# A selective scan with its states taken two at a time: product, C load, accumulating transfer and sum

## Chip, cores and metric

The kernel runs on one core of one Trainium2 chip. The metric is device time in microseconds of one execution. The engines are TensorE (PE, with its weight loads PEld), VectorE (DVE), ScalarE (ACT), GpSimd (POOL) and SyncE (SP); 16 DMA engines serve the core.

## What is computed

The reference takes x of shape (16, 192, 64, 64) through four layers, each behind a normalisation: a small per-channel network that gives a likelihood, a shifted 1x1 convolution (five shifts), a two-dimensional selective scan, and a depthwise convolution with a 1x1 convolution and a batch norm. The change is in the scan:

```
dts, Bs, Cs = split(einsum('bkdl,kcd->bkcl', xs, x_proj_weight))     # 4 directions k, 16 states n
delta = softplus(einsum('bkrl,kdr->bkdl', dts, dt_projs_weight) + bias)
def step(h, inp):                      # over l = 0 .. 4095
    dA = exp(d[..., None] * A)
    h = dA * h + (d * u)[..., None] * Bt[:, :, None, :]
    y = einsum('bkdn,bkn->bkd', h, Ct)
ys = ys + xs * Ds                      # skip
y = sum of the four directions, each brought back to image order
```

The scan's input xn is x2 normalised, (x2 - gm) * rstd, and the kernel adds x2 itself to the scan's result.

## The kernel before, in words

The 16 images go through in eight pairs: 2 x 192 channels are 384 rows, three tiles (j) of 128 partitions. The first tile holds the first image, the third the second, and the middle one 64 rows of each.

A pair's scan (`scans`) runs over 48 steps t: tile j, direction k in the order 1, 3, 0, 2, and a quarter of the 4096 places (LC = 1024). Each step has 16 states n. One state of one step is a slot s, 768 a pair, 6144 in all. In a slot:

- ScalarE makes dA = exp(delta * A) (`decay`, three slots ahead; three buffers).
- TensorE spreads B's row over the partitions into PSUM (`spread`, two slots ahead; two buffers), two bf16 matmuls of 512 columns.
- VectorE multiplies it with du in place (`product`) and scans (`scan`, line 1020): h = dA * h + that.
- ScalarE copies the scan's last column to `state`.
- GpSimd multiplies h with C's row (line 1024). That row has been broadcast over the partitions by a DMA from SyncE's queue (`load_c`, two slots ahead, four buffers `cb`): 512 KB with runs of 4 KB. In the middle tile there are two transfers, one for each 64 partitions.
- Of every four states the first is added to the second by an accumulating DMA from GpSimd's queue (line 1026, 512 KB). The other three are added on TensorE by an identity matmul into PSUM (`add_up`, LATE = 4 slots after the scan), two fp32 matmuls of 512 columns each; the profile shows each fp32 matmul as two records. There are eight buffers of h.
- In the slot of each group's first state `add_up` adds images instead (`images`): for k = 0 the image of x2 (`xc`, a load of its own), the skip term (a diagonal matrix `skip` times xn) and the transposed directions `Xt`; for k = 2 and 3 what the directions before left in X or Xt.
- After the last state ScalarE copies the sum to X or Xt. This PSUM tile has one buffer, which the next step's delta (`step_rest`, at n = 4 and 10) uses too.

The instructions stand in an order written out by hand: each recorded call keeps its place in the program (line 66 in the profile is that recorder). Between these calls run pieces of the next image pair's first layers (`front`: statistics, `layer0`, `layer1`, `project`, `split`), about one piece a slot, paid by a credit; one slot of each step pays none. The eighth pair has no such work. `layer0` copies rows by SyncE to m0, takes tanh on ScalarE and matmuls on TensorE, through t1 and t2; its last matmul on t2 is issued a unit later.

After the scans, `layer3` normalises, convolves (taps on TensorE, GpSimd with ScalarE, and VectorE) and prepares the first step of the next pair (`begin`). Its tiles lie where the scans' buffers were; a tile `gap` of 25 KB keeps the images xp0 and xp1 beyond the scans' own buffers, so that both can be loaded before the scans end.

Pools that share a place in SBUF make the later writer wait for the earlier reader.

Of the kernel before, what the change touches and what calls it, by code (L numbers as in the profile page):

```python
# [11 lines left out]
F32 = mybir.dt.float32  # L12
# [31 lines left out]
LATE = 4  # L44
# [8 lines left out]
GAP = 25  # L53
# [53 lines left out]
def conv_preact_kernel(ctx: ExitStack, tc: tile.TileContext, a: dict):  # L107
# [43 lines left out]
    dtw = const.tile([32 + RD, K, NT, P], F32, name="t_dtw")  # L151
    for r in (0, 32):
        nc.sync.dma_start(out=dtw[r : r + RD], in_=a["dtw"])
# [11 lines left out]
    skip = const.tile([P, NT, P], F32, name="skip")  # L165
# [11 lines left out]
    for j in range(NT):  # L177
        nc.vector.tensor_scalar(skip[:, j, :], ident, dsk[:, 0, j : j + 1], None, ALU.mult)
# [126 lines left out]
    class Made:  # L305
        def __init__(self, n):
            def d(name, shape, dtype=F32):
                return dram.tile(shape, dtype, name=f"{name}{n}")

            self.x2 = d("x2_d", [NT * P, L])  # L310
            self.b = d("b_d", [P, L])
            self.c = d("c_d", [P, L])
            self.dt = d("dt_d", [K * RD, L])

            self.bp = d("bp_d", [K, BP, L], BF16)
            self.cp = d("cp_d", [2 * 2 * N, L])
            self.dtp = d("dtp_d", [2 * RD, L])
            self.gm = const.tile([P, NT], F32, name=f"gm{n}")
            self.rstd = const.tile([P, NT], F32, name=f"rstd{n}")

# [38 lines left out]
    def group_norm(E, st, stat, ps, gm, rstd, tiles=range(NT)):  # L359
# [50 lines left out]
        E.gps.tensor_tensor(rstd, d2, half, ALU.pow)  # L410


    def front(i, o, E, ps, deep):

        with tc.tile_pool(name="f_st", bufs=1) as stat:
            sts = [stat.tile([P, NT, 8, 6], F32, name=f"fst{n}") for n in range(3)]
# [35 lines left out]
            yield from layer1(o, E, ps, deep, sts[2], gms[1], rstds[1])  # L452
            yield from group_norm(E, sts[2], stat, ps, o.gm, o.rstd)
# [4 lines left out]
    def layer0(i, E, ps, deep, st, gm, rstd):  # L458
        with tc.tile_pool(name="l0w", bufs=1) as w_, tc.tile_pool(name="l0x", bufs=3) as xk, tc.tile_pool(
# [11 lines left out]
            def stream(chunks, no):  # L471
# [116 lines left out]
                for u, (ci, q) in enumerate(units):  # L588
# [13 lines left out]
                    t2 = tk.tile([GR, 2, 512], F32, name="t2", tag=f"t2{no}")  # L602
# [37 lines left out]
    def layer1(o, E, ps, deep, st, gm, rstd):  # L640
        with tc.tile_pool(name="l1w", bufs=1) as w_, tc.tile_pool(name="l1x", bufs=2) as xk, tc.tile_pool(
            name="l1r", bufs=6
# [24 lines left out]
            def load_r(c):  # L667
                if c < 8:
                    for j in range(NT):
                        xrs[c, j] = rk.tile([P, 512], F32, name="l1_xr")  # L670
                        E.sp.dma_start(
                            out=xrs[c, j], in_=row_tiles(x1_d)[:, j, 512 * c : 512 * c + 512]
                        )
# [23 lines left out]
            load_r(0)  # L697
# [4 lines left out]
            for c in range(8):  # L702
                at = 0
                for jo in range(NT):
                    p = ps("l1_p")
                    n, last = 0, 5 * len(INTO[jo]) - 1
                    for b, ji in INTO[jo]:
                        for s, (dy, dx) in enumerate(((0, 0), (0, 1), (0, -1), (1, 0), (-1, 0))):
# [11 lines left out]
                            if at == 8:  # L720
                                load_r(c + 1)
# [10 lines left out]
    def project(o, E, ps):  # L732

        with tc.tile_pool(name="pjw", bufs=1) as w_, tc.tile_pool(name="pjx", bufs=3) as xk:
# [21 lines left out]
            def done(to, c, m, p):  # L756
# [4 lines left out]
                E.sp.dma_start(out=to[:, 512 * c : 512 * c + 512], in_=r)  # L761
# [34 lines left out]
    def split(o, E):  # L796

        with tc.tile_pool(name="sp1", bufs=1) as one, tc.tile_pool(name="sp2", bufs=2) as two:
            nat = one.tile([P, L], F32, name="nat")
            E.sp.dma_start(out=nat[0:64, :], in_=o.b[0:64, :])  # L800
            E.sp.dma_start(out=nat[64:128, :], in_=o.c[0:64, :])
# [19 lines left out]
            for m in range(NC_):  # L821
# [3 lines left out]
                ct = two.tile([P, LC], F32, name="ct")  # L825
# [3 lines left out]
                E.sp.dma_start(out=o.cp[:, cs], in_=ct[64:128, :])  # L829
# [23 lines left out]

    def load_dt(sp, o, k, at):
# [9 lines left out]
    def make_delta(E, v, delta, dt, k, j):  # L864

        for h in range(2):
            rows = slice(32 * h, 32 * h + RD)
            E.pe.matmul(
                v[:, 512 * h : 512 * h + 512], dtw[rows, k, j, :], dt[rows, :], start=True, stop=True
# [4 lines left out]
    def load_first(o):  # L874
# [6 lines left out]
        return xn, load_bp(nc.sync, o, k, 0), dt  # L881

    def begin(o, loaded, psum):
# [3 lines left out]
        xn, bp, dt = loaded  # L887
        normalise(nc.vector, xn, xn, o.gm, o.rstd, 0)
        delta = over.tile([P, LC], F32, name="delta", tag="delta", bufs=2)
        make_delta(E, psum(), delta, dt, k, 0)  # L890
        du = over.tile([P, LC], F32, name="du", tag="du", bufs=2)
        nc.gpsimd.tensor_tensor(image(du), image(delta), columns(xn)[:, : LC // HW, :], ALU.mult)
        return xn, bp, delta, du

    def scans(i, o, p3, st3, begun, nxt):

        E = _Engines(tc, True)
        with ExitStack() as es:
# [5 lines left out]
            hp = pool("l2h", 8)  # L904
            da = pool("l2a", 3)
            cp = pool("l2c", 4)
# [5 lines left out]
            Xt = one.tile([P, L], F32, name="Xt")  # L912

# [7 lines left out]
            xns, xcs, state, bps, dts, made, ysum = {}, {}, {}, {}, {}, {}, {}  # L921
# [13 lines left out]
            def next_dt(t):  # L935
                if t < T:
                    j, k, at, first = todo[t]
                    dts[t] = load_dt(E.sp, o, k, at)

# [13 lines left out]
            def load_xc(t):  # L953
                if t < T and todo[t][1] == 0:
                    j, k, at, first = todo[t]
                    xcs[t] = one.tile([P, LC], F32, name="xc")
                    E.sp.dma_start(out=xcs[t], in_=row_tiles(o.x2)[:, j, at : at + LC])

            def load_c(s):
                t, n = divmod(s, N)  # L960
                j, k, at, first = todo[t]
                cb = cbs[s] = cp.tile([P, LC], F32, name="cb")
                src, row = (o.c, 64 + 16 * k) if k % 2 == 0 else (o.cp, 16 * (k - 1))
                for b, rows in {
# [4 lines left out]
                    r = row + N * b + n  # L969
                    E.sp.dma_start(  # L970
                        out=cb[rows, :],
                        in_=src[r : r + 1, at : at + LC].to_broadcast([rows.stop - rows.start, LC]),
                    )

            def step_rest(t):
# [5 lines left out]
                make_delta(E, v, delta, dts.pop(t), k, j)  # L981
# [28 lines left out]
            def scan(s):  # L1010
# [4 lines left out]
                dA, pbt, cb = dAs.pop(s), pbs.pop(s), cbs.pop(s)  # L1015
                back = k >= 2
                flip = slice(None, None, -1) if back else slice(None)
                h = hs[s] = hp.tile([P, LC], F32, name="h")
# [5 lines left out]
                E.gps.tensor_tensor(h, h, cb, ALU.mult)  # L1024
                if n % 4 == 1:
                    E.gps.dma_start(out=h, in_=hs[s - 1], accum_op=ALU.add)

            def add_up(s):

                t, n = divmod(s, N)  # L1030
                if s < 0:
                    return
                j, k, at, first = todo[t]
                if n % 4 == 0:
                    for c in range(LC // 512):
                        for w, v in images(t, n // 4 - 1, 512 * c):
                            E.pe.matmul(
                                ysum[t][:, 512 * c : 512 * c + 512], w, v, start=False, stop=False
                            )
                    return  # L1040
                h = hs.pop(s)
                if n % 4 == 1:
                    hs.pop(s - 1)
                if n == 1:
                    ysum[t] = py.tile([P, LC], F32, name="ysum", tag="ysum")
                for c in range(LC // 512):
                    cs = slice(512 * c, 512 * c + 512)
                    E.pe.matmul(
                        ysum[t][:, cs], ident, h[:, cs], start=(n == 1), stop=(n == N - 1)
                    )  # L1050
                if n == N - 1:
                    if k % 2:
                        E.act.copy(Xt[:, at : at + LC], ysum.pop(t))
                    else:
                        E.act.copy(rows_of(at, LC), image(ysum.pop(t)))

            def images(t, which, c):
# [3 lines left out]
                if k == 0:  # L1061
                    of = [
                        (ident, lambda: xcs[t][:, c : c + 512]),
# [9 lines left out]
                return [(w, v()) for w, v in of[which : which + 1]] if which >= 0 else []  # L1073
# [10 lines left out]
            xns[0], bps[0], *made[0] = begun  # L1084
            next_dt(1)
            for s in range(3):
                decay(s)
            for s in range(2):
                load_c(s)
                spread(s)  # L1090
            fr = front(*nxt, E, ps, False) if nxt is not None else iter(())
# [11 lines left out]
            for s in range(total):  # L1103
                t, n = divmod(s, N)
                j, k, at, first = todo[t]
                if s + 2 < total:
                    load_c(s + 2)
                if n == 2:
                    next_bp(t + 1)
                if n == 4:  # L1110
                    next_dt(t + 2)
                if n == 11:
                    load_xc(t + 1)
# [5 lines left out]
                if n == 4:  # L1119
# [8 lines left out]
                if (t + 1) % (K * NC_) == 0 and 5 <= n < 5 + NC_:  # L1128
                    norm_xn(j + 1, n - 5)
                if n > 4:  # L1130
# [317 lines left out]
```

## Time and profile before

| what | us |
|---|---|
| median of 3 runs | 27460.9 (27457.2 to 27462.78) |
| the profiled execution | 27459.08 |
| its span, first to last instruction | 27457.3 |
| busy: PE / DVE / ACT / POOL | 23391.4 / 23876.2 / 16298.7 / 20528.5 |
| first scan to last scan, pairs 1 to 7, mean | 2911.8 |
| the same, pair 8 | 2765.6 |
| last scan of a pair to first of the next | 342 |

A group's line gives the source line, engine, operation, what is written and read, shapes and count; then busy time, the mean of one in ns, and the engine's idle time just before such instructions with what ended it. A queue's line gives packets, MB, and the time its packets took as a share of 16 engines' span; q0 is GpSimd's queue, q1 SyncE's. A stretch's line gives start and end, length, busy time of each engine with its count, the granted TensorE clock, the share of the DMA engines and GB/s. The trace also records every DMA packet with its queue, size and time; where "packet records" are named, those are meant.

### The profile page before, as it was taken

The numbers are of one execution on the slowest core, as the hardware profiler recorded it, in microseconds if no ns is written. First come the engines' busy times: TensorE is split into PE (matmuls) and PEld (weight loads), VectorE is DVE, ScalarE is ACT, GpSimd is POOL, SyncE is SP. The second block draws the span as 40 slices with busy tenths as digits, with TensorE's granted clock in tenths as the row PEclk, the third lists the DMA queues.
The fourth block names the chain that finished last, engine by engine and source line by source line (L and its number), as shares of the span: only waits on it lengthen the run. The fifth ranks groups of instructions, "written<-read, shape, count | busy, mean of one in ns | idle before, by whom it ended". The sixth has DMA issues, their size and how long they took to land. (4 is left out here: it accounts for less than half of the span.)

```text
span 27457.3 us, 209986 instructions
## 1 busy us (share of the span) xinstructions
PE 23391.4 (85%) x58036; PEld 9490.8 (35%) x58036; DVE 23876.2 (87%) x15098; ACT 16298.7 (59%) x23334; POOL 20528.5 (75%) x10322
## 2 busy tenths in 40 slices
PE   8799888998789987999879988899878998766663
PEld 4343333333333332333334333333333333222221
DVE  0399998999889998999989999899989999899994
ACT  7388555874568644785447845587456864444443
POOL 2388876888778876888768887788877887677772
PEclk9899998999899998999989999999989999888886
DMA  4489874898668974898748987489856897467765
GB/s 102 132 221 226 220 226 131 224 219 218 181 182 225 222 213 142 221 224 224 218 138 220 227 219 220 138 222 218 219 173 188 225 222 215 137 190 194 202 186 245
DMA packets 2009593, 5471.86 MB, mean 199 GB/s; under 512 B 551592, under 2 KB 551816, under 8 KB 1991008
## 3 DMA queue, kind: packets, MB, share of 16 engines
q1 hardware_dynamic: 1783776, 4592.80, 57.7%
q0 software_dynamic: 221184, 805.40, 15.4%
q10 hardware_dynamic: 3456, 60.21, 0.5%
q8 instruction: 463, 7.59, 0.1%
q14 instruction: 714, 5.85, 0.1%
HBM read 3908.47 MB, written 340.96 MB: 155 GB/s over the span
## 5 line engine op out<-in xcount | busy, mean ns | idle before, releaser
L66 POOL TENSOR_TENSOR h<-h,cb 128x1024 f32<-128x1024 f32 x6144 | 14812.9, 2465 | 4331.0 <-ACT state L66 3637.1
L66 DVE TENSOR_TENSOR_SCAN h<-dA,state,pbt 128x1024 f32<-128x1024 f32 x4608 | 10807.6, 2345 | 727.0 <-ACT dA L66 119.9
L66 PE MATMUL ysum<-h,ident 128*128 128x512 f32 x18432 | 9280.1, 628 | 171.6 <-DMA h<-h 119.1
L66 DVE TENSOR_TENSOR pbt<-du,pbt 128x1024 f32<-128x1024 f32 x6144 | 7433.2, 1210 | 569.1 <-PE pbt L66 412.6
L66 ACT ACTIVATE dA<-delta,t_alog 128x1024 f32<-128x1024 f32 x6144 | 7034.6, 1146 | 6.5
L66 PEld LDWEIGHTS ysum<-h,ident 128*128 128x128 f32 x18432 | 3692.8, 202 | 4379.4 <-issue 3858.9
L66 ACT COPY state<-h 128x1 f32<-128x1 f32 x6144 | 1143.3, 186 | 6161.7 <-DVE h L66 6143.2
L66 PE MATMUL pbt<-bp,pick 96*128 96x512 bf16 x8192 | 2623.4, 404 | 1888.0 <-DVE h L66 1867.3
L66 DVE TENSOR_TENSOR_SCAN h<-dA,pbt 128x1024 f32<-128x1024 f32 x1536 | 3507.1, 2283 | 218.9 <-ACT dA L66 38.8
L66 PE MATMUL p<-t,wts 96*128 96x512 f32 x5376 | 2730.7, 605 | 162.8 <-ACT t L66 161.9
L66 PE MATMUL p<-m,wms 128*96 128x512 f32 (+1 forms) x5376 | 2662.4, 596 | 58.9 <-ACT t L66 44.7
L66 ACT ACTIVATE t<-p,bias 96x512 f32<-96x512 f32 x2688 | 1804.2, 678 | 1200.8 <-PE p L66 1187.6
L66 PEld LDWEIGHTS <-pick 96*128 96x128 bf16 x8192 | 673.7, 100 | 4795.4 <-DVE h L66 3281.0
L1209 POOL TENSOR_TENSOR l_g<-l_g,l_m 128x1024 f32<-128x1024 f32 x672 | 1627.5, 2423 | 620.9 <-ACT l_g L1205 474.7
L66 PE MATMUL l_p<-l_xp,w1s 128*128 128x512 f32 x3920 | 1883.3, 596 | 0.0
L66 PE MATMUL pbt<-bp,pick_mix 96*128 96x512 bf16 x4096 | 1270.1, 392 | 560.0 <-DVE h L66 555.5
L66 POOL DMA_DIRECT2D h<-h x1536 | 1356.3, 883 | 495.4 <-POOL h L66 419.3
L66 PEld LDWEIGHTS p<-t,wts 96*128 96x128 f32 x5376 | 1012.1, 191 | 1323.2 <-issue 883.4
L66 ACT ACT_TABLE_LOAD x1082 | 1388.2, 1283 | 19.0
L66 PEld LDWEIGHTS p<-m,wms 128*96 128x96 f32 (+1 forms) x5376 | 941.0, 177 | 811.8 <-issue 355.7
L1232 DVE SCALAR_TENSOR_TENSOR l_p<-xp,wc,l_p 128x1024 f32<-128x1024 f32 x768 | 990.4, 1290 | 223.8 <-PE l_p L1226 198.1
L66 ACT ACTIVATE m<-m,bias,sp 96x512 f32<-96x512 f32 x1344 | 1077.6, 802 | 87.0 <-DMA m<-l_xn 85.1
(241 smaller groups left out, 18647.7 us busy)
## 6 DMA issues: line engine op xcount, KB each, us to landing
cb<-cp_d SPq DMA_DIRECT2D x2048, 512.0 KB
cb<-c_d SPq DMA_DIRECT2D x2048, 512.0 KB
h<-h POOLq DMA_DIRECT2D x1536, 512.0 KB, 7.4
cb<-cp_d SPq DMA_DIRECT2D x2048, 256.0 KB
cb<-c_d SPq DMA_DIRECT2D x2048, 256.0 KB
m<-l_xn SPq DMA_DIRECT2D x3072, 128.0 KB
bp<-bp_d SPq DMA_DIRECT2D x384, 192.0 KB
rl<-x_d ACTq DMA_DIRECT2D x24, 2450.0 KB
```

The costliest lines, as they stand in the source:

```text
L66: return self._tc.keep_in_program_order(call(*args, **kw))
L1209: nc.gpsimd.tensor_tensor(g, g, m, ALU.add)
L1232: nc.vector.scalar_tensor_tensor(image(y if tap is TAPS[-1] else ps), window(j, 16 * c, 16, tap), factor(j, tap), image(ps), ALU.mult, ALU ...
```

## The change

States are taken in twos, u = s // 2:

- h and cb are tiles of 2 x 1024 columns (five of h, three of cb). Each scan writes its half. GpSimd multiplies both halves in one instruction after the second scan.
- C's rows are stored by quarters (`o.c`, `o.cp` get a leading axis of four), so that two states of a quarter lie together, and one load brings 8 KB runs for both. The middle tile still has two loads, of 64 partitions.
- Of every four states the first two are added to the last two by one accumulating transfer of 1 MB; TensorE adds two of four states. The sums come SUM = 6 slots after the scan, the second half one slot later, and images in the two slots between groups.
- For k = 0 the x2 image and the skip term become one image: since x2 = xn * std + gm, the diagonal is dsk + std (`gain`, made anew for each pair by one GpSimd and three ScalarE instructions), and gm is the bias of ScalarE's copy of the sum. `group_norm` makes std by one more GpSimd instruction. The loads `xc` are gone.
- Places in the slot order: dt loads at n = 8, delta at 7, du at 11, normalising the next xn at 4, 5, 8, 9, the slot without credit is 8.
- Room is made: dt's weights are loaded for each tile and direction (two loads of 12 rows), t2 takes the place of m0, `fst` has two tiles, `l1_xr` five with their loads spread out, `ct` one. xp1 lies ahead of a `gap` of 19 KB, over the place of the last h, of dA and of the first cb.

```diff
-LATE = 4
+SUM = 6
-GAP = 25
+GAP = 19
...
-                    t2 = tk.tile([GR, 2, 512], F32, name="t2", tag=f"t2{no}")
+                    t2 = m0[:GR]
...
+    def load_dtw(sp, k, j):
+        w = over.tile([32 + RD, P], F32, name="dtw", tag="dtw", bufs=2)
+        for r in (0, 32):
+            sp.dma_start(out=w[r : r + RD, :], in_=a["dtw"][:, k, j, :])
+        return w
...
-            hp = pool("l2h", 8)
+            hp = pool("l2h", 5)
             da = pool("l2a", 3)
-            cp = pool("l2c", 4)
+            cp = pool("l2c", 3)
...
-            def load_c(s):
-                t, n = divmod(s, N)
+            def load_c(u):
+                t, n = divmod(2 * u, N)
                 j, k, at, first = todo[t]
-                cb = cbs[s] = cp.tile([P, LC], F32, name="cb")
+                cb = cbs[u] = cp.tile([P, 2 * LC], F32, name="cb")
...
                     r = row + N * b + n
+                    two = src[at // LC, r : r + 2, :].rearrange("r l -> (r l)").unsqueeze(0)
                     E.sp.dma_start(
-                        out=cb[rows, :],
-                        in_=src[r : r + 1, at : at + LC].to_broadcast([rows.stop - rows.start, LC]),
+                        out=cb[rows, :], in_=two.to_broadcast([rows.stop - rows.start, 2 * LC])
                     )
...
-                h = hs[s] = hp.tile([P, LC], F32, name="h")
+                u, of = divmod(s, 2)
+                if of == 0:
+                    hs[u] = hp.tile([P, 2 * LC], F32, name="h")
+                h = hs[u][:, LC * of : LC * of + LC]
...
                 E.act.copy(v, h[:, 0:1] if back else h[:, LC - 1 : LC])
-                E.gps.tensor_tensor(h, h, cb, ALU.mult)
-                if n % 4 == 1:
-                    E.gps.dma_start(out=h, in_=hs[s - 1], accum_op=ALU.add)
+                if of:
+                    E.gps.tensor_tensor(hs[u], hs[u], cbs.pop(u), ALU.mult)
+                    if u % 2:
+                        E.gps.dma_start(out=hs[u], in_=hs[u - 1], accum_op=ALU.add)
...
+                turn = (s - SUM - 3) % 4
+                if turn < 2:
+                    t, n = divmod(s - SUM - turn, N)
+                    if t < 0:
+                        return
+                    u = (s - SUM - turn) // 2
+                    if n == 3 and turn == 0:
+                        ysum[t] = py.tile([P, LC], F32, name="ysum", tag="ysum")
                     for c in range(LC // 512):
+                        cs = slice(512 * c, 512 * c + 512)
+                        E.pe.matmul(
+                            ysum[t][:, cs],
+                            ident,
+                            hs[u][:, LC * turn + 512 * c : LC * turn + 512 * c + 512],
+                            start=(n == 3 and turn == 0),
+                            stop=(n == N - 1 and turn == 1),
+                        )
...
+                            elif k == 0:
+                                E.act.activation(
+                                    rows_of(at, LC),
+                                    image(ysum.pop(t)),
+                                    AF.Identity,
+                                    bias=o.gm[:, j : j + 1],
+                                )
...
-                        (ident, lambda: xcs[t][:, c : c + 512]),
                         (skip[:, j, :], lambda: xns[j][:, at : at + 512]),
...
+            E.gps.tensor_tensor(gain, dsk[:, 0, :], o.std, ALU.add)
+            for j in range(NT):
+                E.act.activation(skip[:, j, :], ident, AF.Copy, scale=gain[:, j : j + 1])
...
-                if s + 2 < total:
-                    load_c(s + 2)
+                if s % 2 == 0 and s + 2 < total:
+                    load_c(s // 2 + 1)
...
+            xp1 = gap.tile([P, S, S], F32, name="xp1")
             gap.tile([P, GAP * 256], F32, name="gap")
             diag = xk.tile([P, NT, PE_TAPS, P], F32, name="diag")
-            xps = [xk.tile([P, S, S], F32, name=f"xp{j}") for j in range(NT - 1)] + [X]
+            xps = [xk.tile([P, S, S], F32, name="xp0"), xp1, X]
```

## The prediction, made before the result was known

> **What bounds the kernel now.** I read first the page's queues and costliest groups, then busy time by stretch, then what VectorE (DVE) waited for, last the end of one pair. A "slot" is one state of one step: one product and one scan on VectorE. There are 768 in a pair and 6144 in all.
>
> ```profile
> q1 hardware_dynamic: 1783776, 4592.80, 57.7%
> q0 software_dynamic: 221184, 805.40, 15.4%
> ...
> L66 POOL TENSOR_TENSOR h<-h,cb 128x1024 f32<-128x1024 f32 x6144 | 14812.9, 2465 | 4331.0 <-ACT state L66 3637.1
> L66 DVE TENSOR_TENSOR_SCAN h<-dA,state,pbt 128x1024 f32<-128x1024 f32 x4608 | 10807.6, 2345 | 727.0 <-ACT dA L66 119.9
> L66 PE MATMUL ysum<-h,ident 128*128 128x512 f32 x18432 | 9280.1, 628 | 171.6 <-DMA h<-h 119.1
> L66 DVE TENSOR_TENSOR pbt<-du,pbt 128x1024 f32<-128x1024 f32 x6144 | 7433.2, 1210 | 569.1 <-PE pbt L66 412.6
> ...
> L66 POOL DMA_DIRECT2D h<-h x1536 | 1356.3, 883 | 495.4 <-POOL h L66 419.3
> ```
>
> A slot costs VectorE 1.21 + 2.33 = 3.55 us whatever else happens, and the change touches neither instruction. GpSimd (POOL) idled 4331 us before its h*C product, most of it waiting for the scan, so that product is not the bound.
>
> The next view is busy time by stretch: the three channel tiles (256 slots each) of the second pair, then of the eighth, which has no next image to prepare. After the stretch and its length come PE, PEld, DVE, ACT and POOL, the granted clock, the share of the DMA engines and GB/s.
>
> ```profile
> 4457.00:5436.00 979.00, 899.25 (x2285) 370.36 (x2286) 911.05 (x558) 745.64 (x1104) 788.50 (x403) 0.96 0.82 226
> 5436.00:6400.00 964.00, 894.50 (x2289) 369.76 (x2288) 906.80 (x547) 682.61 (x1007) 812.40 (x419) 0.98 0.95 224
> 6400.00:7363.00 963.00, 816.38 (x2021) 323.06 (x2019) 911.79 (x564) 470.82 (x681) 751.33 (x381) 0.95 0.77 223
> 23981.00:24902.00 921.00, 623.84 (x1410) 226.78 (x1411) 887.32 (x519) 402.25 (x585) 697.13 (x336) 0.87 0.67 195
> 24902.00:25825.00 923.00, 632.40 (x1426) 233.22 (x1425) 888.84 (x521) 401.37 (x584) 699.21 (x337) 0.87 0.79 194
> 25825.00:26746.00 921.00, 635.41 (x1432) 234.07 (x1431) 887.49 (x524) 394.63 (x581) 696.08 (x341) 0.86 0.67 196
> ```
>
> The reader sees that without a next image VectorE is 96% busy and a slot takes 921/256 = 3.60 us; with one, slots take 3.82, 3.77 and 3.76. From first scan to last, the first seven pairs take 2911.8 us on average and the eighth 2765.6. Of the 146 us between them, 66.5 are VectorE's own work for the next image (72 statistics at 0.68, 24 sums at 0.73). So 2911.8 - 2765.6 - 66.5 = 80 us a pair, 0.10 a slot, is waiting that a better order could remove: 560 us in seven pairs is the ceiling of any gain in the scans, and the floor of a slot is 3.60 + 0.09 = 3.69. The second tile already fills the DMA engines to 0.95.
>
> ```profile
> DVE pbt L66 <- PE pbt L66: 412.6, 553, 4.2
> ...
> DVE h L66 <- ACT dA L66: 158.7, 491, 2.7
> ...
> DVE h L66 <- DMA h<-h: 137.6, 90, 5.9
> ```
>
> VectorE's largest wait in the scans is for TensorE's spread of B. So TensorE, 92 to 93% busy in the first two tiles, is the second bound.
>
> **Part by part.** *Sums on TensorE.* Eight of 16 states (12 before) reach TensorE: 18432 records become 12288. Four that follow each other took 1.88 us in the timeline, 0.43 apart, so 6144 x 0.43 = 2640 us of TensorE go, 0.43 a slot of some 3.6; the dropped x image takes 384 records, 165 us. That empties the queue in front of the spread, and the 413 us of waits should go. What is late next is VectorE itself (floor 3.69) where nothing else binds.
>
> *Accumulating transfers.* They stay 1536 but carry 1 MB: 805 MB become 1611. A 4 KB packet of this queue took 341 ns on average in the packet records (a C-load packet 159 in the median). A slot has two on each DMA engine; doubled, +0.68 us of each engine's time per slot. No packet of 8 KB is accumulated in this trace: between 1.9 and 2.1 times 341; I take 2.0. GpSimd's issue (0.88 us) stays the same in number; if rows are cut into 4 KB pieces it may double, +0.22 us a slot of an engine that is 80 to 84% busy: 0 taken.
>
> *C loads in 8 KB runs.* Bytes are the same. The trace's nearest 8 KB packets (instruction fetch) took 309 ns at the tenth percentile against 2 x 159: -0.04 us a slot. The first packet of each transfer takes 300 to 450 ns instead of 159, and transfers halve: I take -0.16 us a slot where a tile has one load per state, -0.26 in the second, where it has two; bounds 0 and -0.35. The Trainium skill ("DMA: Bandwidth & Descriptors", section "Anatomy of one DMA") puts about 2 us of fixed cost on each transfer, measured on GpSimd's queue: 2 x 3.2 us become 4.4, an estimate, 2 us saved for two states, or 6 ms over the kernel were it on the path. The row says it isn't: GpSimd waited 605 us for C loads in all, 49 of it at the start of the second pair alone. I count only the engine time.
>
> *Where both meet.* The same page ("Issuing engines are not separate DMA queues") says that transfers issued by sync and by GpSimd run on the same 16 engines and interleave. This speaks against the change: work leaves TensorE for engines that the C loads need. Were the accumulating queue separate, I would take the floor everywhere (27020, below). The trace agrees with the page: in 20 us stretches of the second tile the shares never add up to much over 1.
>
> ```profile
> 2360.00:2380.00 20.00, 19.60 (x51) 8.08 (x49) 19.39 (x12) 18.15 (x27) 19.48 (x11) 1.00 1.06 238
> ```
>
> So I take 1.04 as full. Time of each engine per slot: first tile 0.82 x 3.82 = 3.13, + 0.68 - 0.04 - 0.16 = 3.61; over 1.04 that is 3.47, under the floor, but close. Third: 0.77 x 3.76 = 2.90, so 3.38; free. Second: 0.95 x 3.77 = 3.58, + 0.68 - 0.04 - 0.26 = 3.96, or 3.81 us a slot; without any saving 4.26, or 4.10. I take the middle, 3.95. The second tile is dear because each half of the partitions has its own load: its C packets took about 260 ns, against 205 in the other tiles. The eighth pair has 0.79 x 3.60 + 0.38 = 3.2 us and doesn't bind.
>
> *Sum of the scans.* First tile 3.82 to 3.73 (a little over the floor, since the engines are nearly full): -23 us. Second 3.77 to 3.95: +47. Third 3.76 to 3.70: -15. Together +9 a pair, x7 = +63 us.
>
> *End of a pair.*
>
> ```profile
> 4114.96 2.34 POOL L66 TENSOR_TENSOR h<-h,cb 128x1024 f32<-128x1024 f32 x1 [1.31 <-ACT state L66]
> ...
> 4127.25 1.03 ACT L66 COPY X<-ysum 128x1024 f32<-128x1024 f32 x1 [12.37 <-PE ysum L66]
> ```
>
> Before, the last sum was read 12.6 us after the last scan (which ended at 4114.66). Now the last two states come in one product (4.6 us: 2.36, and 2.14 per further 1024 columns, by the rows of 512 and 1024), then issue and landing (6.5 us in the eighth pair, + 8 x 0.33), then 8 records of 0.43 to 0.6: copy at about 4133. Nothing covers it, since statistics and group norm follow: +6 us x 8 = +48.
>
> *Waits that arise.* The sum now waits for a larger transfer, six slots after the scan instead of four. From scan to landing took 14 us (first tile) and 15 (second) in the median, against 15.1 allowed. Now: lag of GpSimd behind the scan 2.9 or 3.9 (medians of before), product 4.6, issue to landing 7.5 or 8.0 plus 2.7 for the bytes and up to 2.5 for interleaved C packets, in all 17.7 to 21.5, against 22.6. Behind a waiting sum on TensorE stands the next spread, but VectorE has two of those in hand, so under 4 us nothing is lost. Five h buffers let a scan start once the transfer of seven slots back has landed: 24 us. Only the second tile's tail reaches this; it is inside my 3.95.
>
> *At no cost:* t2 in m0's place makes SyncE's row copies wait for the closing matmul of the last unit; behind them stand C loads, which have some 18 us; TensorE passes that matmul in the same slot. dtw loads, gain and skip (one GpSimd and three ScalarE instructions a pair, under 2 us), std, and later delta and du (five slots of cover) go the same way. xp1 now lies over the last h, dA and C buffers, so its load starts with the last scan; it needs about 8 us and is first used 25 us later. If a cover failed, each would cost 2 to 8 us a pair, 16 to 64 us.
>
> Sum: 27459 (the profiled execution; span 27457.3; median of the runs 27460.9) + 63 + 48 = 27570.
>
> **Rivals.**
> A, likeliest (0.45): as summed; own range 27420 to 27800, the savings' bounds in the second tile. If rows are cut back into 4 KB (the change then doesn't do what it says), 4.10 there: 27459 + 7 x (84 - 38) + 48 = 27830.
> B, faster (0.33): the packet times are waiting rather than work, the engines overlap, and TensorE's relief counts everywhere. All slots at 3.70: 7 x 768 x (3.70 - 3.79) = -484, + 48: 27020; half of it 27265. For it: the second tile's first quarter (5436 to 5670) ran at 3.66 a slot with a DMA share of 0.97. Against it: the change asks for a tenth more than that.
> C, much slower (0.22): the engines bind in the first tile too and landings come after the 24 us of the h buffers, deciding once the landing is over 16 us from issue. Slots 3.95, 4.15, 3.76: 7 x (33 + 97) + 48: 28420; milder, 28000.
>
> **Numbers.** 27570; the range takes B to 27100 and C to 28150. Over or under 0.2% (55 us) is what a measurement can tell from no change. Faster: B and a little of A, 0.34; same: 0.13; slower: the rest of A, and C, 0.53.
>
> **What would show it.** ysum<-h x12288 and VectorE's waits for the spread below 100 us: the TensorE step. Queue 0 at about 30% of 16 engines: the transfer step; near 25%, B. DMA share of the second tile at 1.0 with slots over 3.85: the saturation; at 3.70, B. X copy 18 us after the last scan: the pair's end. Waits of scans for h<-h over 500 us: C. I am wrong if an 8 KB packet costs far from 2 x 341 ns, or if C packets shrink when their engines are full.

## The result and the profile after

The changed kernel takes 29257.2 us (median of 4 runs, 29233.0 to 29319.1) where the kernel before, in the same comparison, took 27459.1 (27452.0 to 27462.8). The ratio is 1.0659, with a 95% interval of 1.064 to 1.0677: 6.6% slower. The sign of the forecast held, its size (+111 us against +1798) did not; the time lies outside the range, past the price given to rival C.

First the page after: queues (packets, MB, share of 16 engines), then the groups that answer to those of before.

```profile
q1 hardware_dynamic: 1317296, 4543.25, 53.7%
q0 software_dynamic: 221184, 1610.71, 27.3%
...
L66 POOL TENSOR_TENSOR h<-h,cb 128x2048 f32<-128x2048 f32 x3072 | 14037.5, 4573 | 6252.2 <-ACT state L66 5242.4
L66 DVE TENSOR_TENSOR_SCAN h<-dA,state,pbt 128x1024 f32<-128x1024 f32 x4608 | 10808.8, 2346 | 2204.5 <-DMA h<-h 1644.9
L66 DVE TENSOR_TENSOR pbt<-du,pbt 128x1024 f32<-128x1024 f32 x6144 | 7425.6, 1209 | 455.5 <-PE pbt L66 280.6
...
L66 PE MATMUL ysum<-h,ident 128*128 128x512 f32 x12288 | 6717.0, 675 | 149.6 <-DMA h<-h 149.6
...
L66 POOL DMA_DIRECT2D h<-h x1536 | 1366.7, 890 | 495.4 <-POOL h L66 456.3
...
h<-h POOLq DMA_DIRECT2D x1536, 1024.0 KB, 11.6
```

Most instructions cost what they cost before or what the sum gave them: the scan 2346 ns (2345), the product of two states 4573 (forecast 4.6 us), the issue 890 (883), and 12288 records of sums, together 2563 us less (forecast 2640), though each takes longer (675 ns, 628 before; see the last section). What is new is what VectorE's scan waits for: 2204 us instead of 727, most of it the accumulating transfer. The waits name it in full (us in all, times, longest):

```profile
DVE h L66 <- DMA h<-h: 2065.4, 719, 11.9
...
DVE pbt L66 <- PE pbt L66: 280.6, 269, 4.9
...
ACT m L66 <- DMA m<-l_xn: 674.1, 196, 10.9
```

Before, the first was 137.6, the second 412.6, and the third stood at

```profile
ACT m L66 <- DMA m<-l_xn: 85.1, 70, 3.7
```

(ScalarE waiting for the rows of the next image that SyncE copies to m0). A scan waits for h<-h for one reason only: the h buffer that it writes is still being read or written by an accumulating transfer.

Busy time by stretch: the three tiles of the second pair, then of the eighth.

```profile
4714.00:5757.00 1043.00, 845.10 (x2011) 334.21 (x2012) 909.54 (x557) 747.50 (x1105) 767.20 (x275) 0.89 0.88 240
5757.00:6873.00 1116.00, 866.66 (x2016) 343.92 (x2015) 903.53 (x547) 688.58 (x1008) 790.31 (x289) 0.87 1.00 220
6873.00:7877.00 1004.00, 754.55 (x1748) 290.91 (x1746) 912.29 (x565) 471.33 (x683) 733.11 (x255) 0.86 0.88 247
25675.00:26643.00 968.00, 580.21 (x1136) 199.61 (x1136) 887.52 (x518) 402.17 (x588) 673.61 (x208) 0.72 0.80 217
26643.00:27567.00 924.00, 574.22 (x1152) 203.35 (x1153) 888.41 (x520) 400.38 (x584) 674.69 (x209) 0.74 1.02 227
27567.00:28544.00 977.00, 591.60 (x1163) 208.31 (x1163) 888.40 (x525) 393.98 (x583) 674.79 (x213) 0.72 0.80 215
```

VectorE's busy time (the third of the five) is unchanged to within 0.4%; its stretches are longer. Slots of pairs 1 to 7 take 4.08, 4.32 and 3.92 us by tile (3.84, 3.77, 3.76 before). All tiles but the second of the eighth pair lost, so saturation of the second tile can't be the whole. The last three lines hold the riddle: in the eighth pair the second tile has the fullest engines (1.02) and the fewest waits, slots of 3.61, while the first and third, at 0.80, take 3.78 and 3.82. VectorE's waits for h<-h in those three stretches:

```profile
DVE h L66 <- DMA h<-h: 53.6, 32, 4.0
...
DVE h L66 <- DMA h<-h: 4.2, 5, 1.3
...
DVE h L66 <- DMA h<-h: 60.1, 30, 4.1
```

The addresses of the h buffers in the built program explain it. A pool of five does not hand its buffers out in turn. In the eighth pair's first and third tiles, the source of an accumulating transfer (an even u) comes round four pairs of states later in 61 of 64 cases (counted by the scan that takes the buffer), its target six later; in the second tile both come round five later in 59 of 64. In pairs 1 to 7, the source has a round of four in 61, 44 and 53 of 64. With a round of four, the scan that takes the buffer starts five slots after the start of the scan that released the transfer: 5 x 3.6 - 2.35 = 15.6 us from that scan's end to the landing. With five it is seven slots: 22.8 us. Landings came 16.2, 19.8 and 16.4 us after the scan in the three tiles (medians). So the tile with the latest landings had room, and the others didn't.

One of these waits in the timeline (start, length, and in brackets the wait):

```profile
26109.17 2.35 DVE L66 TENSOR_TENSOR_SCAN h<-dA,state,pbt 128x1024 f32<-128x1024 f32 x1 [1.62 <-DMA h<-h]
```

By stretch, pairs 1 to 7 lost 7 x (3152.8 - 2911.8) = 1687 us between first and last scan, pair 8 103, what lies between and around them 17.

### The profile page after: what moved, and what is told of

The parts are those of the page before. It is cut to its first block, busy times and chain, and to the rows that moved or that the text cites. A ratio compares the mean times of both kernels' runs of the same rounds, so it can differ in the third digit from the quotient of the medians.

```text
span 29264.2 us, 182538 instructions
## 1 busy us (share of the span) xinstructions
PE 22247.3 (76%) x51508; PEld 8757.2 (30%) x51508; DVE 23846.3 (81%) x15095; ACT 16341.4 (56%) x23358; POOL 20043.6 (68%) x7266
## 3 DMA queue, kind: packets, MB, share of 16 engines
q0 software_dynamic: 221184, 1610.71, 27.3%
## 5 line engine op out<-in xcount | busy, mean ns | idle before, releaser
L66 POOL TENSOR_TENSOR h<-h,cb 128x2048 f32<-128x2048 f32 x3072 | 14037.5, 4573 | 6252.2 <-ACT state L66 5242.4
L66 DVE TENSOR_TENSOR_SCAN h<-dA,state,pbt 128x1024 f32<-128x1024 f32 x4608 | 10808.8, 2346 | 2204.5 <-DMA h<-h 1644.9
L66 DVE TENSOR_TENSOR pbt<-du,pbt 128x1024 f32<-128x1024 f32 x6144 | 7425.6, 1209 | 455.5 <-PE pbt L66 280.6
L66 PE MATMUL ysum<-h,ident 128*128 128x512 f32 x12288 | 6717.0, 675 | 149.6 <-DMA h<-h 149.6
L66 PE MATMUL pbt<-bp,pick 96*128 96x512 bf16 x8192 | 2878.2, 438 | 3561.5 <-DVE h L66 3502.8
L66 PEld LDWEIGHTS ysum<-h,ident 128*128 128x128 f32 x12288 | 2717.5, 222 | 3390.1 <-issue 3123.0
L66 PE MATMUL p<-m,wms 128*96 128x512 f32 (+1 forms) x5376 | 2980.5, 660 | 58.1 <-ACT lu L66 50.7
L66 PE MATMUL l_p<-l_xp,w1s 128*128 128x512 f32 x3920 | 2075.1, 649 | 11.8 <-POOL l_xp L66 11.8
L66 PE MATMUL p<-m,wts 96*128 96x512 f32 x2688 | 1492.7, 672 | 187.1 <-ACT m L66 185.8
L66 PE MATMUL p<-t,wts 96*128 96x512 f32 x2688 | 1477.4, 632 | 0.0
L66 ACT ACT_TABLE_LOAD x1082 | 1388.2, 1283 | 17.6
L66 PEld LDWEIGHTS <-pick_mix 96*128 96x128 bf16 x4096 | 360.2, 103 | 3295.3 <-DVE h L66 1832.5
L66 ACT ACTIVATE t<-p,bias 96x512 f32<-96x512 f32 x1344 | 900.4, 682 | 553.8 <-PE p L66 544.2
## 6 DMA issues: line engine op xcount, KB each, us to landing
h<-h POOLq DMA_DIRECT2D x1536, 1024.0 KB, 11.6
```

Source lines behind the costliest of these rows:

```text
L66: return self._tc.keep_in_program_order(call(*args, **kw))
```

## The experiments

Slots are us by tile, mean of pairs 1 to 7, then of pair 8.

| kernel | us | ratio to before, 95% | slots, pairs 1 to 7 | slots, pair 8 |
|---|---|---|---|---|
| before | 27459 | | 3.84 3.77 3.76 | 3.60 3.60 3.60 |
| after | 29257 | 1.064 to 1.0677 | 4.08 4.32 3.92 | 3.78 3.61 3.82 |
| e1, five in turn | 28449 | 1.0343 to 1.0374 | 3.91 4.20 3.79 | 3.59 3.62 3.60 |
| e9, rounds of 4 and 6 | 29570 | 1.0753 to 1.0782 | 4.08 4.38 3.97 | 3.82 4.00 3.81 |
| e5, e1 with C in 4 KB runs | 28560 | 1.0387 to 1.0415 | 3.96 4.23 3.82 | 3.59 3.60 3.60 |
| e6, e1 without half loads | 27789 | 1.0098 to 1.0129 | 3.93 3.83 3.79 | 3.59 3.60 3.60 |
| e8, e1 without the transfers | 27266 | 0.9914 to 0.9941 | 3.78 3.76 3.76 | 3.59 3.59 3.58 |
| e10, e1 with bytes of before | 27674 | 1.0066 to 1.0093 | 3.87 3.84 3.80 | 3.61 3.61 3.62 |
| e2, half transfer, two h read | 33485 | 1.2174 to 1.2211 | 4.73 4.73 4.81 | 4.66 to 4.70 |
| e3, before with t2 in m0 | 27534 | 1.0018 to 1.0037 | 3.84 3.81 3.77 | |
| e4, before with every second state transferred | 27978 | 1.0168 to 1.0202 | 3.84 4.00 3.79 | 3.63 3.64 3.62 |
| e7, before with eight in turn | 27386 | 0.9959 to 0.9982 | 3.81 3.77 3.76 | 3.60 3.60 3.60 |

**e1: the changed kernel, h buffers in turn**

```diff
-                    hs[u] = hp.tile([P, 2 * LC], F32, name="h")
+                    hs[u] = hp.tile([P, 2 * LC], F32, name="h", tag=f"h{u % 5}", bufs=1)
```

> The changed kernel, with one edit: its five h buffers are handed out strictly in turn. In the program of the changed kernel the source of an accumulating transfer is handed out again four pairs of states later (61 of 64 times in tiles 1 and 3 of pair 8), so its next scan may start only when a transfer of five slots back has landed; strictly in turn it is seven slots. Theory H (this hand-out is what costs): pair 8 returns to 3.60 us a slot in every tile (now 3.78, 3.61, 3.82), the scans' 2065 us of waits for h<-h fall below 300, tiles 1 and 3 with a next image go to 3.70 to 3.78 (now 4.08 and 3.92), in all 27400 to 27900. Theory D (the DMA engines are full): pair 8 changes, but with a next image tile 2 stays above 4.1 a slot (now 4.32) and tile 1 above 3.9, waits go over to the C loads and row copies; 28300 to 29000.

Measured: 28449.1, so 808 us of the 1798 come back with one argument. The wait for the transfer falls to an eighth; what grows in its place is the scans' wait for TensorE's read of the buffer (11.0 in the changed kernel) and ScalarE's for the row copies:

```profile
DVE h L66 <- PE ysum L66: 686.1, 430, 16.1
...
DVE h L66 <- DMA h<-h: 243.1, 74, 8.5
...
ACT m L66 <- DMA m<-l_xn: 1145.2, 295, 17.2
```

Pair 8 returns to 3.59 to 3.62 in all tiles, as theory H had it; the other pairs and the whole stay where theory D had them. The second tile of those pairs stays dear at 4.20. Its stretches in the second pair, by tile:

```profile
4595.00:5591.00 996.00, 825.79 (x2018) 328.63 (x2019) 909.25 (x558) 751.61 (x1110) 767.95 (x276) 0.92 0.92 252
5591.00:6663.00 1072.00, 858.86 (x2010) 337.78 (x2009) 904.39 (x546) 682.44 (x1004) 787.94 (x288) 0.89 1.02 230
6663.00:7631.00 968.00, 741.58 (x1743) 287.14 (x1742) 908.41 (x563) 471.01 (x681) 732.16 (x254) 0.88 0.90 254
```

The engines are full in the second tile, as forecast, and move fewer bytes a second there (230 against 252) than in the first. In the eighth pair, which has no row copies and no other loads for a next image, the same tile shows a share of 1.03 at slots of 3.62:

```profile
25858.00:26784.00 926.00, 575.46 (x1152) 204.26 (x1152) 888.62 (x521) 400.31 (x585) 675.80 (x209) 0.74 1.03 226
```

There the full engines just meet what is asked, 1.03 x 3.62 = 3.73 us a slot; with a next image it is 1.02 x 4.20 = 4.28, which fits in no slot of 3.7.

**e9: rounds of four and six in every tile**

```diff
-            hp = pool("l2h", 5)
+            he, ho = pool("l2he", 2), pool("l2ho", 3)
...
-                    hs[u] = hp.tile([P, 2 * LC], F32, name="h")
+                    hs[u] = (ho if u % 2 else he).tile([P, 2 * LC], F32, name="h")
```

> The changed kernel with its h buffers split: two for even u, three for odd u, so that in all tiles a source tile of an accumulating transfer comes round four pairs later and a target six. Theory (the round of the buffers is what the second 808 us are): tile 2 of the eighth pair, which had rounds of five and slots of 3.61, now gets rounds of four and slots of 3.80 or more (50 us or more); in pairs 1 to 7 the 20 of 64 groups of tile 2 and 11 of 64 of tile 3 that had five follow (4.37 and 3.95 a slot, 100 and 50 us). In all 29460 us. Rival (turns of five helped for another reason, such as which places in memory are written together): 29257 as the changed kernel, tile 2 of pair 8 at 3.61.

Measured: 29570.3, dearer than the change itself. The eighth pair, its second tile in the middle:

```profile
25860.00:26837.00 977.00, 580.99 (x1136) 199.55 (x1136) 887.44 (x519) 401.18 (x588) 672.51 (x208) 0.72 0.81 215
26837.00:27859.00 1022.00, 591.11 (x1152) 204.48 (x1152) 887.76 (x520) 400.26 (x584) 675.60 (x209) 0.71 0.95 206
27859.00:28832.00 973.00, 584.06 (x1158) 203.95 (x1159) 886.57 (x525) 393.61 (x582) 674.77 (x213) 0.72 0.80 215
```

The second tile went from 924 to 1022 us (slots 3.61 to 4.00) when only the round of its buffers changed; the first and third, which had rounds of four already, stayed. Second and third tile of the other pairs came to 4.38 and 3.97, as expected; that the whole is 110 us over the expected 29460 lies half in the eighth pair's second tile, which lost 98 us instead of 50. So the round causes the waits; that its price follows the landing is seen too: 5 x 4.00 - 2.35 = 17.6 us, near the 18.4 us at which landings came there.

**e5: C loads cut back to 4 KB runs, and e6: no loads of 64 partitions.** Both start from e1.

```diff
-                    two = src[at // LC, r : r + 2, :].rearrange("r l -> (r l)").unsqueeze(0)
-                    E.sp.dma_start(
-                        out=cb[rows, :], in_=two.to_broadcast([rows.stop - rows.start, 2 * LC])
-                    )
+                    for of in range(2):
+                        E.sp.dma_start(
+                            out=cb[rows, LC * of : LC * of + LC],
+                            in_=src[at // LC, r + of : r + of + 1, :].to_broadcast(
+                                [rows.stop - rows.start, LC]
+                            ),
+                        )
```

> The kernel with five buffers strictly in turn (28449 us; tile 2 at 4.20 us a slot with a next image), and its C loads again in runs of 4 KB: two transfers into the halves of the same buffer. Theory R: in tile 2, where each half of the partitions has its own load[...] (a C packet of 8 KB took 565 to 575 ns there, two of 4 KB 500 in the kernel before with doubled accumulation); tile 2 returns to 4.0 and the whole to 28000 to 28200. Rival: half as many transfers was a saving, as the prediction had it (0.16 to 0.26 us a slot); without it tile 2 goes to 4.4 and the whole to 28700 or more.

```diff
-                    1: ((0, slice(0, 64)), (1, slice(64, P))),
+                    1: ((0, slice(0, P)),),
```

> The kernel with five buffers strictly in turn, where the middle tile takes the first image's C for all 128 partitions in one transfer, so that 64 of its rows get another image's C; the work and bytes are the same. If the two half transfers are what makes tile 2 dear: C packets there fall from 565 to about 385 ns, tile 2 goes from 4.20 to 3.85 to 3.92 like tile 1, the whole to 27800 to 28000. If it is the work of the next image that stands beside tile 2 (its first layer's end and its second layer): packets fall, but tile 2 stays above 4.1.

Measured: e5 28560.5, 111 us over e1. The long runs do save, 0.03 to 0.04 us a slot in each tile, but they are not what loads the second tile: its C packets took 279 to 286 ns for 4 KB in e5 (means of pairs 1 to 7), about half of the 563 to 572 for 8 KB in e1. Neither theory R (28000 to 28200) nor its rival (28700 or more) is met. e6 took 27789.1, 660 us less than e1; its C packets in the second tile 384 to 393 ns, the slot 3.83. The second tile of its second pair:

```profile
5490.00:6471.00 981.00, 828.34 (x2013) 332.50 (x2012) 903.32 (x547) 684.82 (x1006) 789.84 (x289) 0.93 0.92 252
```

So two loads of 64 partitions, at equal bytes, take nearly half more packet time than one of 128, and with the engines full this is paid: 660 of e1's 990 us. Why they do is not shown. The number of transfers is not it, since e5 doubles that for 0.03 us a slot; but e6 also reads one row of C for all partitions where e1 reads two, and no run separates this from the split.

**e8: no accumulating transfers, and e10: those of before**

```diff
-                    if u % 2:
-                        E.gps.dma_start(out=hs[u], in_=hs[u - 1], accum_op=ALU.add)
```

> The kernel with five buffers strictly in turn, without the accumulating transfers: the first two of every four states are left out of the sum, all else stays. Theory D: 1.3 us of DMA engine time per slot goes, and tile 2 falls from 4.20 to 3.70 to 3.80, tile 1 from 3.91 to 3.70 to 3.75; the whole 27000 to 27350, which is what TensorE's relief would give with a free sum. If other parts (row copies behind t2, C loads in twos) hold the slots: tile 2 stays above 3.9, the whole above 27700.

e10 is e1 with these lines, and a sum of the even pair's second half one slot ahead of the other two:

```diff
-                    if u % 2:
-                        E.gps.dma_start(out=hs[u], in_=hs[u - 1], accum_op=ALU.add)
+                    if u % 2 == 0:
+                        E.gps.dma_start(out=hs[u][:, LC:], in_=hs[u][:, :LC], accum_op=ALU.add)
```

> The kernel of e1 (five h buffers in turn) with the traffic of before: the transfer adds only the first state of each even pair to the second, 512 KB, within one buffer, and TensorE adds three of four states, the additional one ahead of the other two. Products, C loads, x and skip stay in twos as in the change. Theory (the bytes of the accumulating transfers are the whole loss): with turns of five and bytes of before it stands near the kernel before in turns, 27386: between 27300 and 27500, VectorE's waits for the spread back at about 400 us. Rival (products and C loads in twos cost by themselves, by releasing h and cb later): over 27700, with waits of scans for h<-h or for ysum over 300 us.

Measured: e8 27266.0, 1183 us under e1: with five in turn, the transfers cost more than the whole loss that is left. With a third of TensorE's sums gone and no transfer paid for them, the kernel gains 193 us on before, 0.7%. The second tile of its second pair:

```profile
5399.00:6363.00 964.00, 819.27 (x2013) 330.13 (x2012) 902.98 (x547) 686.85 (x1006) 731.87 (x225) 0.94 0.84 188
```

e10 took 27673.7, between the times that theory and rival had expected; its waits are the rival's. Halving the bytes and giving TensorE its third state back gains 775 us on e1, so the doubled transfers are the main cost. Not all of it need be bytes: in e10 source and target are one buffer, so each transfer also holds fewer buffers. The bytes without that are in e4, below (520 us). 288 us over e7 remain in e10 with the bytes of before. Its longest wait in the scans:

```profile
DVE h L66 <- PE ysum L66: 699.3, 523, 9.2
```

Buffers of two states, released in twos and late, hold up the scans. The waits for the spread, expected back at 400 us, did not come back (92 us), so e10 waits for buffers where the kernel before waited for the spread. How the 288 us divide is not settled: t2 in m0's place (76 us in e3, below) is among them, and the second tile's C loads take 584 to 593 ns for 8 KB there, with a share of 0.98 where e7 has 0.94.

**e2: half the transfer, from two h buffers**

```diff
-                        E.gps.dma_start(out=hs[u], in_=hs[u - 1], accum_op=ALU.add)
+                        E.gps.dma_start(out=hs[u][:, LC:], in_=hs[u - 1][:, LC:], accum_op=ALU.add)
...
+                        if turn == 0:
+                            E.pe.matmul(
+                                ysum[t][:, cs], ident, hs[u - 1][:, cs], start=(n == 3), stop=False
+                            )
```

> As the kernel with five buffers strictly in turn, and the accumulating transfer is 512 KB again: only the second of two states is accumulated, and TensorE adds three of four states as before the change. Product and C load stay in twos. Theory D: this takes 0.68 us of DMA engine time per slot away, tile 2 returns to 3.8, and the kernel is 500 us or more faster than with the whole transfer, 27300 to 27700. Theory H: with strict turns the transfer's size costs little; the kernel is within 200 us of the one with the whole transfer, or slower, since TensorE is full again (waits for the spread back to about 400 us).

Measured: 33484.5. This experiment failed as a test of the bytes: TensorE now reads the first of the two buffers nine slots after its first scan, and the buffer is wanted after ten. VectorE waited 6621.6 us for it (1500 times). It shows only how dear a late release is; e10 was made in its place.

**e3, e4, e7: parts put into the kernel before.** e3 is the one line `t2 = m0[:GR]`; e7 is `tag=f"h{s % 8}", bufs=1` on its h; e4 takes TensorE's sums from twelve to eight of 16 states by twice as many transfers of 512 KB:

```diff
-                if n % 4 == 1:
+                if n % 2:
                     E.gps.dma_start(out=h, in_=hs[s - 1], accum_op=ALU.add)
...
+                if n % 2 == 0:
+                    return
```

> The kernel before, with one edit of the change alone: t2 lies in m0. Theory T: SyncE's row copies now wait for the closing matmul of the unit before, and C loads stand behind them; ScalarE's wait for the copied rows goes from 85 us to 400 or more and the kernel becomes 100 to 500 us slower, 27560 to 27960. Rival: the copies have two slots of cover, under 50 us of change, 27410 to 27510.

> The kernel before, with the doubled accumulating traffic alone, in pieces of 512 KB: every odd state is accumulated from the even one before it, TensorE adds eight of 16 states. C loads, product, sums four slots later and buffers stay as before. Theory D: DMA share of tile 2 goes to 1.03 or more and its slots from 3.77 to 3.95 to 4.2; the whole 27600 to 28300, whatever the buffers do. Theory H: a transfer of 512 KB lands in 8 us, eight buffers suffice, and TensorE's relief shows: tile 1 from 3.84 to 3.70, the whole 26950 to 27350.

> The kernel before with one edit: its eight h buffers are handed out strictly in turn (in its program some are handed out again after five to seven states). Theory H for the kernel before: VectorE's 138 us of waits for h<-h go, 27330 to 27430. Rival: those waits stand beside others, no change, 27440 to 27480.

Measured: e3 27534.2, 76 us slower, with ScalarE's wait for the row copies at 233.2 us instead of 85.1. e4 27978.4, 520 us slower, the second tile at 4.00 with a share of 1.02: the doubled bytes load the engines without any of the change's other parts (GpSimd issues twice as often there, and the pool's own rounds stay). e7 27386.0, 81 us faster than the kernel before in the same comparison (27467.5), because there too the pool's rounds were uneven (five to nine, where eight was meant), and VectorE's 137.6 us of waits for h<-h are gone from the trace. Ratio 0.997, interval 0.9959 to 0.9982: of the kernels that compute the whole result it is the fastest.

## Why the prediction was wrong

In steps of the medians, 27461 to 29257 (the kernel before stood between 27458 and 27467 in the comparisons that they come from): turns in the kernel before, -75 (e7); pairs with the bytes of before, +288 (e10); doubled bytes for a third of TensorE's sums, +775 (e1); the pool's own rounds, +808. The steps are not independent, but each is a kernel that ran.

**The step that failed first** is "Five h buffers let a scan start once the transfer of seven slots back has landed: 24 us. Only the second tile's tail reaches this". It counted the buffers and took it that they go round in turn. For most sources the seven slots were five, and the 24 us were 5 x 3.76 - 2.35 = 16.5. The time to landing was forecast rightly, 17.7 to 21.5 us (medians of 16.9 to 21.5 in the second pair), and was itself already over that: with the true round, the prediction's own numbers give waits in the first two tiles. The runs showed 2065 us of such waits, and 808 us that turns alone took back. The order in which the program's buffers get their places could be read before any run; the number of buffers is not that order.

**The second is a term of the sum that was mis-sized:** the second tile at 3.95 us a slot, measured 4.20 with the turns right. The engine time asked for there is 1.02 x 4.20 = 4.28 us; the forecast had 3.96, and "without any saving 4.26". So the 0.30 us that longer C runs were to save did not come. By the packets, this tile's C loads took 8 x 0.26 = 2.08 us of each engine a slot before, 4 x 0.567 = 2.27 in e1 and, cut back to 4 KB, 8 x 0.283 = 2.26 in e5: they rose by 0.2 instead of falling by 0.3, whatever the run, and the slot of e5 is only 0.03 us dearer. The prediction had named C packets that shrink when the engines are full as a sign of being wrong; they grew. Its working was generous, too: half of what a first packet takes over the 159 ns is 0.07 to 0.15 us for one load a state, where 0.16 was taken. The accumulating packet was sized rightly: 648 ns on average for 8 KB, forecast 682; queue 0 stands at 27.3%, forecast about 30.

**The third is the first and third tile,** forecast 3.73 and 3.70, measured 3.91 and 3.79 with turns. The demand was right (0.92 x 3.91 = 3.60; forecast 3.61), but "free" under 1.04 was not: at 0.92 slots already stretch. e8, without any such transfers, has 3.78 and 3.76 there, so the floor of 3.69, taken from the eighth pair, was not to be had in this form either; of the first tile's 0.18 over forecast, 0.05 is this and 0.13 comes with the transfers. Which wait carries the 0.13 is not settled: landings, row copies (1145 us) and TensorE's late reads all grew.

**Point by point.** VectorE's waits for the spread fell, to 280.6, not under 100. "At no cost" for t2 was wrong by 76 us, somewhat over the 64 that the text allowed for a failed cover. The end of a pair: the copy to X came 18 us after the last scan, as forecast, but the gap to the next pair's first scan stayed at 342 (342.7). The 6 us were right in themselves: in e4 the copy comes 18.9 us after the last scan and the gap is 348.3. In the changed kernel another piece moved out of the way. Before, VectorE normalised the next pair's xn after the group norm, 34 to 35 us after the last scan in each pair:

```profile
4148.44 4.43 DVE L341 TENSOR_SCALAR xn<-xn,gm,rstd 128x4096 f32<-128x4096 f32 x1
```

Now it starts 0.3 to 2.5 us after the last scan, inside the wait for the copy, which gives some 4.4 us back. So most of the +48 was not paid; after the last pair, which has no next xn, the end grew from 711 to 720. That the sign of the forecast held is in part luck, then: of the terms behind its +111, saturation of the second tile was right in kind, but most of the 48 was not paid, and the 38 us a pair to be won in the other two tiles were not won.

**The rivals.** C named the right place, landings against h buffers, with waits of scans "over 500 us" as its sign; it had 2065. Its deciding point, "over 16 us from issue", was too high by the same error as the first step: the median from issue was 11.6 us. It was given 0.22. B had VectorE at 3.70 everywhere: e8, without any transfers, gains 193 us, so B's 27020 was out of this kernel's reach even then. The rule that the prediction took from the Trainium skill ("DMA: Bandwidth & Descriptors", section "Issuing engines are not separate DMA queues"), that transfers of both issuers run on the same engines, spoke for a loss and was borne out: ScalarE's wait for SyncE's row copies is 84.9 us without GpSimd's transfers (e8), 245.4 with those of before (e10) and 1145.2 with doubled ones (e1). The same page's 2 us a transfer ("Anatomy of one DMA") would have made 6 ms, an estimate, had it been on the path; the prediction left it out, and halving the number of C loads was worth 111 us (e5 against e1).

## What to carry to other kernels

A buffer pool of n gives room for n only if its buffers go round in turn; read the places in the built program, count the slots to the next writer for the tile that is held longest, and set that against the landing time. Here one argument was worth 808 us in the changed kernel and 75 to 81 in the one before. Work taken from a busy engine pays only as far as that engine set the end (193 us here, with no transfers at all), and work given to engines at 0.82 to 0.95 of their time can cost before they reach 1: with the next image's loads beside it, a share of 0.92 went with slots of 3.91, while without them 1.03 went with 3.62. Cover for a transfer should be counted in slots between named instructions, not in buffers.

## What the runs showed of the hardware

- TensorE's granted clock was lower with fewer sums: 0.938 before, 0.859 after, and in the eighth pair 0.72 to 0.74 instead of 0.86 to 0.87; with the third state back (e10) it was 0.929. A record of the sum took 675 ns instead of 628 on average. Sums and the x image were to take 2805 us from TensorE; its busy time fell by 1144 (23391.4 to 22247.3). Part of the relief is thus given back in slower matmuls. The Trainium skill ("TensorE: Matmul & The Clock Gate", section "The HAM clock gate") says that the clock is gated unless the engine has been busy; these rows agree in direction, and the clock records of the traces know only full and half clock, half for 3416 us before and 8265 after. The share of busy time alone doesn't set it: e2, with TensorE busy for 74% of its span, had 0.900, the changed kernel with 76% had 0.859.
- Two loads of 64 partitions, from two rows, cost the engines more than one of 128 from one row, at equal bytes: C packets of 8 KB took 563 to 572 ns against 384 to 393 (e1, e6), and 591 to 597 with no accumulating transfers at all (e8), where the second tile at a share of 0.84 had slots as short as the others (3.76).
- An accumulated packet takes about double with its size: 341 ns for 4 KB, 648 for 8 KB.
